# A stack of four graph layers: maps back to node-major on the quarters of the TensorE array, and sums over nodes on four column tiles

## The chip, the cores and the metric

The kernel runs on one core of one Trainium2 chip. The metric is the device time of one execution in microseconds; lower is better. The median of three runs of the kernel before is 1238.32 us (1236.02 to 1239.87). The profile was taken in an execution of 1238.1 us, of which the traced span is 1236.1 us.

## What is computed

The input `x` has 8 batches of 2048 nodes with 64 features in fp32, and `adj` is a 2048x2048 matrix of which each row is divided by its number of entries. Four layers follow each other. Each one takes a layer norm and a ReLU, applies a graph layer, and adds the result to `x`:

```python
h = relu(layernorm(x)); x = x + L0(h, adj)   # Chebyshev convolution: h, adj h, adj adj h with node-wise weights
h = relu(layernorm(x)); x = x + L1(h, adj)   # three steps: v = W2 relu(W1 [v, adj v] + b1) + b2
h = relu(layernorm(x)); x = x + L2(h, adj)   # adj h, scaled per feature, times w_out, plus b_out
h = relu(layernorm(x)); x = x + L3(h, adj)   # attention over adj > 0.5, softmax over nodes, elu
```

Before layer 1 begins, node 0 of `v` is set to a given vector (`L1_gnn_intervention_value`). Where no entry of `adj` is above 0.5, which is the case with these inputs, the attention of layer 3 comes out uniform, and the layer is a mean over all nodes and an elu of it. The kernel's main path is made for that case. A test of that case runs beside the other work; a general path stands behind a flag and isn't entered here.

## The kernel before

Two batches are held side by side, so that one item is a pair of batches: 2 x 64 features fill the 128 partitions or columns of a tile. There are four items (`NP`), and each is cut in four blocks of 512 nodes (`NB`). The pattern of the adjacency lies in SBUF for the whole run as `BT`.

Data has two forms. *Node-major* tiles hold 128 nodes on the partitions, four such groups in a block, and the 128 features of the pair in the columns. *Feature-major* tiles hold the 128 features on the partitions and 512 nodes in the columns. The big product (`product`, L245 to L256) goes from node-major to feature-major: for each of 16 chunks of nodes it multiplies a high and a low half of the data (`halves`, L225) with `BT`, 32 matmuls of 128x512 that all add up in one PSUM bank. The layers run 4 items x 4 blocks of it in several stages. `fill` puts other TensorE work after chosen chunks.

`back_to_nodes` (L661) goes from feature-major to node-major and applies a 64x64 weight matrix to both batches on the way. The weight tile `wmat` is 128x128 with the same 64x64 matrix in two corners on the diagonal and zeros elsewhere. For each of the four groups of 128 nodes the feature-major tile is the stationary operand and `wmat` the moving one. It is called

- in `prepare_next` (L672) for each block of an item that enters layer 1 (16 calls, PSUM tile `bn_u`): a block of `h` is loaded, in block 0 node 0 is overwritten with `ivt` (L681, a copy of one row on ScalarE), the block is transposed, copied to SBUF, mapped back and split into halves;
- in `finish` of `layer1` (L876) for each block of each of the three steps (48 calls, `bn`);
- in `finish2` of `layer2` (L946) for each block (16 calls, `bn`).

Another small map of layer 1, `map_two` (L894, PSUM tile `ph`), stays feature-major. It already addresses the four 64x64 quarters of the array, with one product of 512 columns on each.

`sums` (L957) is the mean of layer 3: for each block it multiplies the four groups of 128 nodes by a 128x128 matrix of ones, 16 products for an item, all adding up in one PSUM tile `pS`. `outputs` (L969) then makes the elu and the final add.

All products of these parts are fp32; each appears in the trace as two matmul records with a weight load each. A scheduling layer orders the instructions of each engine from the program's order, priorities and dependences; `tc.issue_after(x)` makes it put an instruction behind `x` on its engine. [...]The order on ScalarE matters for one point of the change: the copy of `ivt` into the next item's block (L681), the ReLU of a block in layer 1 (L918), the copies of `ph` (L907) and the casts in `halves` (L230) share its queue.

PSUM tiles come from three tags with two buffers each: `big` (two banks), `mm` and `tr` (one bank).

Of the kernel before, what the change touches and what calls it, by code (L numbers as in the profile page):

```python
# [8 lines left out]
F32 = mybir.dt.float32  # L9
# [4 lines left out]
AF = mybir.ActivationFunctionType  # L14
ALU = mybir.AluOpType
# [27 lines left out]
def uniform_path(  # L43
# [30 lines left out]
    nc = tc.nc  # L74
    P = 128
    B, N, C = x.shape
    NP = B // 2
    NCH = N // P
    NB = N // 512
# [6 lines left out]
    psums = [pro.enter_context(tc.tile_pool(name="psump", bufs=1, space=bass.MemoryType.PSUM))]  # L86
# [14 lines left out]
    def bank(tag, name):  # L101
        return psums[-1].tile([P, 512], F32, tag=tag, name=name)
# [11 lines left out]
    ones = consts.tile([P, P], F32, name="ones")  # L114
# [19 lines left out]
    def nodes(acc):  # L134

        return acc.rearrange("p j f -> p (j f)").rearrange("p (e j c) -> p j e c", e=2, c=C)

    def load_x(layer, p, nb, queue=nc.sync):
        acc = block("acc", f"acc_{layer}_{p}_{nb}", 2)
        fill_x(acc, layer, p, nb, queue)  # L140
        return acc
# [6 lines left out]
    def load_h(p, nb, name, pool):  # L148
        t = pool.tile([P, 4, 2 * C], F32, tag="hb", name=f"hb_{name}", bufs=2 if lastp else 3)
        (nc.sync if lastp else nc.scalar).dma_start(t, hs[p][:, part(nb), :])  # L150
        return t
# [9 lines left out]
    def split(t):  # L161
        return t.rearrange("p j (b c) -> p j b c", b=2)
# [8 lines left out]
    squares, lows, stored = [], [], []  # L171
# [50 lines left out]
    copies = []  # L222
    lastp = []

    def halves(src, name, pool=None, later=None):  # L225

        pool, bufs = (work, 6) if pool is None else (pool, 4)
        Hq = pool.tile([P, 4, 2 * C], F32R, tag="H", name=f"H_{name}", bufs=bufs)
        Lq = pool.tile([P, 4, 2 * C], F32R, tag="L", name=f"L_{name}", bufs=bufs)
        copies.append(nc.scalar.copy(Hq, src))  # L230
        def rest():
            lows.append(nc.vector.tensor_tensor(Lq, src, Hq.bitcast(F32), op=ALU.subtract))

        rest() if later is None else later.append(rest)
        return Hq, Lq
# [29 lines left out]
    def to_feat(h, out, name):  # L265
        pt = transposed(lambda t: h[:, t, :], name)
        nc.scalar.copy(out, pt.rearrange("p t n -> p (t n)"))
        return out
# [7 lines left out]
    def term(k, name):  # L276
        pool = l0t if k == 1 else l0f[0]
        return pool.tile([P, 512], F32, tag=f"t{k}", name=name, bufs=(2, 4, 1)[k])
# [286 lines left out]
    nm = "0_1_3a"  # L565
    tx = work.tile([P, 512], F32, tag="z", name=f"t1T_{nm}", bufs=3)
    ps = bank("b1", f"bv_{nm}")
    for m in range(NCH):
        if m in (2, 7, 12):
            go_back(1 + m // 5)  # L570
        for i in range(2):
            nc.tensor.matmul(
                ps, hls[1][m // 4][i][:, m % 4, :], BT[:, m, 3 * 512:],
                start=(m == 0 and i == 0), stop=(m == NCH - 1 and i == 1),
# [32 lines left out]
    b1c = consts.tile([P, 1], F32, name="b1c")  # L607
    b1s = consts.tile([P, 1], F32, name="b1s")
# [43 lines left out]
    w1e = consts.tile([P, P], F32, name="w1e")  # L652
    ivt = consts.tile([1, P], F32, name="ivt")

    def feat(i, name):

        if i == 0:
            return term(1, name)
        return lastp[0].tile([P, 512], F32, tag="fm", name=name, bufs=4)

    def back_to_nodes(fT, wmat, name, tag="big"):  # L661

        ps = psums[-1].tile([P, 4, 2 * C], F32, tag=tag, name=f"bn_{name}")
        for t in range(4):
            nc.tensor.matmul(ps[:, t, :], fT[:, t * P:(t + 1) * P], wmat, start=True, stop=True)  # L665
        return ps


    items = [(1, p) for p in range(NP)] + [(2, p) for p in range(NP)]
    ops = {}  # L670

    def prepare_next(n, q):  # L672
        if n >= len(items):
            return
        layer, p = items[n]
        nm = f"{layer}_{p}_{q}"
        hl, gT = ops.setdefault(n, ([], []))
        h = load_h(p, q, nm, lastp[0] if n else l0q)
        if layer == 1:
            if q == 0:  # L680
                nc.scalar.copy(h[0:1, 0, :], ivt)  # L681
            gT.append(to_feat(h, feat(0, f"gT_{nm}"), nm))
            h = back_to_nodes(gT[q], w1e, f"u_{nm}", "big" if n else "mm")
        hl.append(halves(h, nm))

    def rows4(r):
        return r.rearrange("p (b c) -> p b c", b=2)[:, None].to_broadcast([P, 4, 2, C])
# [47 lines left out]
    for p in range(NP):  # L735
# [47 lines left out]
        for nb in range(NB):  # L783
            nm = f"0_{p}_{nb}b"
# [4 lines left out]
                tag="mm" if p + nb else "b0",  # L789
# [32 lines left out]
    w1vT, w1eT, w2T, wos, w1v2, w1e2, r1e, rbo = (wl[:, i, :] for i in range(8))  # L822
# [46 lines left out]
    def layer1(n, p):  # L869
        hl, gT = ops[n]  # L870
        steps = 3
        for s in range(steps):
            last = s == steps - 1
            g_new, hl_new = [], []

            def finish(nb):  # L876
                nm = f"1_{p}_{s}_{nb}"
                if last:
                    acc = load_x(1, p, nb)
                    pn = back_to_nodes(g_new[nb], w2T, nm)  # L880
                    nc.vector.tensor_tensor(nodes(acc), split(pn), nodes(acc), op=ALU.add)
                    keep(p, nb, acc, f"2_{p}_{nb}", rows4(rbo))
                else:
                    pn = back_to_nodes(g_new[nb], w1e2, nm)
                    nc.vector.tensor_tensor(split(pn), split(pn), rows4(r1e), op=ALU.add)
                    hl_new.append(halves(pn, nm))

            def mid():
                if last:
                    prepare_next(n + 1, 2)  # L890
                else:
                    finish(2)

            def map_two(nb):  # L894

                ph = psums[-1].tile([P, 2, 512], F32, tag="big", name=f"ph_1_{p}_{s}_{nb}")
                w = w1v2 if s else w1vT
                two = (slice(0, C), slice(C, P))
                for i in range(2):
                    for bb in range(2):  # L900
                        nc.tensor.matmul(  # L901
                            ph[two[bb ^ i], bb, :], w[two[bb], two[bb]], gT[nb + i][two[bb], :],
                            start=True, stop=True,
                        )
                for i in range(2):
                    for bb in range(2):
                        nc.scalar.copy(gT[nb + i][two[bb], :], ph[two[bb ^ i], bb, :])  # L907

            for nb in range(NB):
                nm = f"1_{p}_{s}_{nb}"  # L910
                crow = load_crow(nb, nm)
                g = feat((s + 1) % 2, f"g_{nm}")
                fill = {8: mid} if nb == 3 else {}
                if nb % 2 == 0:
                    fill[10] = lambda: map_two(nb)
                product(hl, nb, nm, g, crow, fill=fill)
                gadd = nc.vector.tensor_tensor(g, g, gT[nb], op=ALU.add)
                nc.scalar.activation(g, g, AF.Relu, bias=b1s if s else b1c)  # L918
                g_new.append(g)
                go_on()  # L920
                if nb in (1, 2):
                    finish(nb - 1)
                    if last:
                        prepare_next(n + 1, nb - 1)
                if s < 2:
                    k = 2 * (8 * p + 4 * s + nb)
                    with tc.issue_after(gadd.ins):
                        test(k)
                        test(k + 1)
            if last:  # L930
                finish(2)
                prepare_next(n + 1, 3)
            if last and n == NP - 1:

                put_off.append(lambda: finish(3))
            else:
                finish(3)
            gT, hl = g_new, hl_new
# [4 lines left out]

    accs, es, zs, pS = [], [], {}, {}

    def finish2(g):  # L946
        p, nb = divmod(g, NB)
        nm = f"acc_2_{p}_{nb}"
        acc = term(1, nm) if p % 2 else feat(1, nm)
        acc = acc.rearrange("p (j f) -> p j f", j=4)  # L950
        accs.append(acc)
        fill_x(acc, 2, p, nb)
        pn = back_to_nodes(es[g], wos, f"2_{p}_{nb}")
        nc.vector.tensor_tensor(nodes(acc), split(pn), nodes(acc), op=ALU.add)
        norm_relu(acc, f"3_{p}_{nb}", lambda h: zs.update({g: h}))

    def sums(g):  # L957
        p, nb = divmod(g, NB)
        if nb == 0:
            pS[p] = bank("tr", f"pS_{p}")  # L960
        for t in range(4):
            nc.tensor.matmul(  # L962
                pS[p][:, :2 * C], ones, zs[g][:, t, :],
                start=(nb == 0 and t == 0), stop=(nb == NB - 1 and t == 3),
            )
        if nb == NB - 1:
            outputs(p)

# [648 lines left out]
```

## Time and profile before

| | |
|---|---|
| time, median of 3 | 1238.32 us |
| span of the trace | 1236.1 us |
| TensorE busy | 1197.7 us, 97% |
| VectorE busy | 744.7 us, 60% |
| ScalarE busy | 237.0 us, 19% |
| GpSimd busy | 223.5 us, 18% |
| matmul records | 5798 |
| granted TensorE clock, mean | 0.993 of full |

A page of the profile lists engines with busy time, the span in slices, DMA queues, the chain of work that ended last, and groups of instructions: line, engine, operation, output and inputs, partitions x elements, count, busy time and mean of one, and the idle time of the engine before them with what ended it. Matmuls are pipelined, so the busy time of a group of matmuls is more than what it adds to the queue. What a group adds is read from the starts of the matmuls around it. In the timeline each row has its start, its time, engine, line and operation; equal neighbours are merged.

By time, layer 0 runs until about 630 us (its last products with the node-wise weights), layer 1 until about 1087 us (its last map back), and layer 2 with the sums of layer 3 to the end; each overlaps a little with the next.

### The profile page before, as it was taken

What the parts mean: (1) busy time and instruction counts of PE and PEld (TensorE: products, weight loads), DVE (VectorE), ACT (ScalarE), POOL (GpSimd) and SP (SyncE); (2) the same over time, 40 slices, a digit from 0 to 9 for tenths busy, and PEclk for the clock granted to TensorE, in tenths of its full rate; (3) what the DMA queues carried; (4) which work ended last, traced back from release to release, by engine and by line L of the source; (5) the groups of instructions that cost most, each with busy time, mean ns of one, the idle gap of its engine ahead of it and who ended that gap; (6) DMA issues with size and microseconds to landing.
All of it is one profiled execution on the core that took longest, in us unless ns stands there. A gap on an engine that the chain in (4) does not pass through costs nothing.

```text
span 1236.1 us, 15662 instructions
## 1 busy us (share of the span) xinstructions
PE 1197.7 (97%) x5798; PEld 843.7 (68%) x5798; DVE 744.7 (60%) x1940; ACT 237.0 (19%) x377; POOL 223.5 (18%) x233
## 2 busy tenths in 40 slices
PE   5899999999999999999989999999999999999995
PEld 4675555555675557655557787787877877888884
DVE  5456888777757774477654436444644545566664
ACT  6610001000010000000022233233223223211100
POOL 5410222211131111011110013003101400331211
PEclk9999999999999999999999999999999999999997
DMA  9951334332332233122256526543743563533311
GB/s 355 379 154 47 102 105 115 84 86 77 90 102 73 64 82 85 54 64 64 60 128 126 134 85 156 132 85 123 158 115 92 154 131 92 155 124 112 119 58 40
DMA packets 100985, 140.99 MB, mean 114 GB/s; under 512 B 43772, under 2 KB 58108, under 8 KB 98852
## 3 DMA queue, kind: packets, MB, share of 16 engines
q1 hardware_dynamic: 82820, 80.74, 24.9%
q0 software_dynamic: 11776, 48.15, 12.9%
q10 hardware_dynamic: 6304, 11.01, 2.8%
q8 instruction: 48, 0.79, 0.3%
q14 instruction: 37, 0.30, 0.1%
HBM read 95.03 MB, written 35.66 MB: 106 GB/s over the span
## 4 chain that ended last, share of the span: by engine, by line
PE 92%; DMA 3%; DVE 3%; issue 1%; POOL 1%; ACT 0%; SPq 0%; POOLq 0%; ACTq 0%
PE bv L250 38%; PE y L711 26%; PE bn L665 5%; PE bv_1b L250 2%; PE bv_3b L250 2%; PE bv_2b L250 2%; PE bv_0b L250 2%; PE ph L901 2%; DMA BT<-in_adj_dram 2%; PE bn_u L665 1%; PE bv_0a L250 1%; PE bv_3a L250 1%; PE pt L262 1%; PE bv_2a L250 1%; PE pS L962 1%; PE bv_1a L250 1%
## 5 line engine op out<-in xcount | busy, mean ns | idle before, releaser
L250 PE MATMUL bv<-BT,H 128*128 128x512 f32 x1024 | 409.7, 400 | 0.0
L250 PE MATMUL bv<-BT,L 128*128 128x512 f32 x1024 | 401.3, 392 | 0.0
L250 PEld LDWEIGHTS bv<-BT,H 128*128 128x128 f32 x1024 | 193.0, 188 | 56.6 <-issue 19.5
L250 PEld LDWEIGHTS bv<-BT,L 128*128 128x128 f32 x1024 | 193.0, 188 | 37.0
L720 DVE SCALAR_TENSOR_TENSOR acc<-y,emb,acc 128x128 f32<-128x128 f32 x512 | 176.3, 344 | 65.7 <-PE y L711 65.7
L720 DVE SCALAR_TENSOR_TENSOR odd<-y,emb,odd 128x128 f32<-128x128 f32 x448 | 153.4, 343 | 0.0
L711 PE MATMUL y<-wt,t0T 64*128 64x512 f32 x512 | 143.7, 607 | 2.4 <-DVE odd L720 1.7
L194 POOL TENSOR_TENSOR rstd<-var,mhalf 128x8 f32<-128x8 f32 x64 | 105.7, 1653 | 182.4 <-DVE var L191 181.0
L240 DVE TENSOR_TENSOR g<-bv,crow 128x512 f32<-128x512 f32 x48 | 33.2, 691 | 173.0 <-PE bv L250 173.0
L186 ACT ACTIVATE sq<-z 128x512 f32<-128x512 f32 x64 | 40.4, 631 | 398.0 <-DVE z L181 388.1
L711 PEld LDWEIGHTS y<-wt,t0T 64*128 64x128 f32 x512 | 45.8, 185 | 63.3 <-issue 57.1
L692 POOL TENSOR_TENSOR acc<-acc,b2r 128x512 f32<-128x512 f32 x16 | 22.2, 1389 | 315.7 <-DVE z L181 315.7
L692 POOL TENSOR_TENSOR acc<-acc,wl 128x512 f32<-128x512 f32 x16 | 20.5, 1283 | 295.8 <-DVE z L181 295.8
L711 PE MATMUL y<-wt,t1T 64*128 64x512 f32 x256 | 66.7, 589 | 0.0
L197 DVE SCALAR_TENSOR_TENSOR z<-z,rstd 128x512 f32<-128x512 f32 x64 | 44.7, 703 | 35.2 <-POOL rstd L194 35.2
L665 PEld LDWEIGHTS bn<-wl,g 128*128 128x128 f32 x384 | 49.8, 193 | 7.5 <-issue 3.0
L665 PE MATMUL bn<-wl,g 128*128 128x128 f32 x384 | 51.5, 277 | 2.6 <-issue 2.6
L189 DVE TENSOR_REDUCE var<-sq 128x8 f32<-128x512 f32 x64 | 43.6, 681 | 15.6 <-ACT sq L186 15.6
L846 DVE SCALAR_TENSOR_TENSOR junk<-mt,cols,st 128x512 uint8<-128x512 bf16 x64 | 47.7, 745 | 2.7 <-DMA mt<-MD 2.3
L907 ACT COPY g<-ph 64x512 f32<-64x512 f32 x64 | 37.2, 581 | 49.6 <-PE ph L901 48.8
L711 PEld LDWEIGHTS y<-wt,t1T 64*128 64x128 f32 x256 | 27.1, 187 | 27.8 <-issue 27.8
L181 DVE TENSOR_TENSOR z<-acc,mean 128x512 f32<-128x512 f32 x56 | 38.3, 692 | 6.0 <-DMA hs<-z 4.6
(213 smaller groups left out, 1649.7 us busy)
## 6 DMA issues: line engine op xcount, KB each, us to landing
BT<-in_adj_dram POOLq DMA_DIRECT2D x16, 1024.0 KB, 19.6
crow<-crowD SPq DMA_DIRECT2D x64, 256.0 KB, 3.4
st<-in_adj_dram SPq DMA_DIRECT2D x64, 256.0 KB, 3.5
hs<-z POOLq DMA_DIRECT2D x40, 256.0 KB, 3.1
xs<-acc POOLq DMA_DIRECT2D x32, 256.0 KB, 2.4
MD<-BT POOLq DMA_DIRECT2D x16, 512.0 KB, 5.6
acc<-xs SPq DMA_DIRECT2D x32, 256.0 KB, 3.9
hb<-hs SPq DMA_DIRECT2D x28, 256.0 KB, 3.5
```

What stands on the lines that cost most here:

```text
L181: firsts.append(nc.vector.tensor_tensor(split(z), nodes(xt), each(mean)[:, :, :, None].to_broadcast([P, 4, 2, C]), op=ALU.subtract))
L186: squares.append(nc.scalar.activation(sq, z, AF.Square))
L189: nc.vector.tensor_reduce(var, groups(sq), axis=AX.X, op=ALU.add)
L194: powers.append(nc.gpsimd.tensor_tensor(rstd, var, mhalf, op=ALU.pow))
L197: scales.append(nc.vector.scalar_tensor_tensor(groups(h), g, 0.0, rstd[:, :, None].to_broadcast([P, 8, C]), op0=ALU.max, op1=ALU.mult))
L250: nc.tensor.matmul(ps, hl[m // 4][i][:, m % 4, :], BT[:, m, nb * 512:(nb + 1) * 512], start=(m == 0 and i == 0), stop=(m == NCH - 1 and i ...
L665: nc.tensor.matmul(ps[:, t, :], fT[:, t * P:(t + 1) * P], wmat, start=True, stop=True)
L692: nc.gpsimd.tensor_tensor(nodes(acc), nodes(acc), more, op=ALU.add)
L711: nc.tensor.matmul(y[:, bb, :], terms[k][hs_, ts], wt[hs_, k, dg * 512:(dg + 1) * 512], start=(k == 0), stop=(k == K - 1),)
L720: last = nc.vector.scalar_tensor_tensor(xj, yd, ec, old, op0=ALU.mult, op1=ALU.add)
L846: nc.vector.scalar_tensor_tensor(junk, mt, cols[:, i, :], st, op0=ALU.mult, op1=ALU.not_equal, accum_out=bad[:, i, q:q + 1],)
L907: nc.scalar.copy(gT[nb + i][two[bb], :], ph[two[bb ^ i], bb, :])
```

## The change

It replaces the 128x128 form of the map back. Since the weight matrix is zero outside its two corners, half of each full product multiplies zeros. The new `back_to_nodes` gives each quarter of the array a 64x64x64 product: the row half is the batch, the column half is a half of the 128 nodes. The two batches go to two banks of a `big` tile, and the result is handed out as a view with the batch as its own axis. `halves` and the adds in `finish` and `finish2` take that view. For item 0 the old form stays as `back_whole`, in a tile of the tag `mm`.

The sums over nodes use four column tiles of 32 columns: each of the four groups of 128 nodes is multiplied by 32 columns of ones on its own tile, so each tile keeps its own partial sum on 32 partitions of `pS`. At the end of an item one row of each of the four is added up by a product with `sel`, a matrix that has ones in the rows 0, 32, 64 and 96; a VectorE copy `four` brings `pS` to SBUF for that. For the last item this is done one block early, and the last block is added with the old form.

A third edit concerns order: the copy of `ivt` into the next item's block is put behind the newest ReLU of layer 1 on ScalarE.

```diff
-    def back_to_nodes(fT, wmat, name, tag="big"):
-        ps = psums[-1].tile([P, 4, 2 * C], F32, tag=tag, name=f"bn_{name}")
+    two = (slice(0, C), slice(C, P))
+    def back_to_nodes(fT, wmat, name):
+        ps = psums[-1].tile([P, 2, 512], F32, tag="big", name=f"bn_{name}")
+        for t in range(4):
+            for hf in range(2):
+                for bb in range(2):
+                    at = t * P + hf * C
+                    nc.tensor.matmul(
+                        ps[two[hf], bb, t * C:(t + 1) * C],
+                        fT[two[bb], at:at + C], wmat[two[bb], two[bb]], start=True, stop=True,
+                    )
+        return ps[:, :, :4 * C].rearrange("p b (t c) -> p t b c", c=C)
+    def back_whole(fT, wmat, name):
+        ps = bank("mm", f"bn_{name}").rearrange("p (t f) -> p t f", t=4)
         for t in range(4):
             nc.tensor.matmul(ps[:, t, :], fT[:, t * P:(t + 1) * P], wmat, start=True, stop=True)
         return ps
...
+    relus = []
...
             if q == 0:
-                nc.scalar.copy(h[0:1, 0, :], ivt)
+                with tc.issue_after(relus[-1].ins) if relus else nullcontext():
+                    nc.scalar.copy(h[0:1, 0, :], ivt)
             gT.append(to_feat(h, feat(0, f"gT_{nm}"), nm))
-            h = back_to_nodes(gT[q], w1e, f"u_{nm}", "big" if n else "mm")
+            h = (back_to_nodes if n else back_whole)(gT[q], w1e, f"u_{nm}")
...
-                nc.scalar.activation(g, g, AF.Relu, bias=b1s if s else b1c)
+                relus.append(nc.scalar.activation(g, g, AF.Relu, bias=b1s if s else b1c))
...
+    sel = lastp[0].tile([P, P], F32, name="sel")
+    nc.gpsimd.memset(sel, 0.0)
+    for q in range(0, P, 32):
+        nc.gpsimd.memset(sel[q:q + 1, :], 1.0)
...
+        final = g + 1 == NP * NB
         if nb == 0:
             pS[p] = bank("tr", f"pS_{p}")
-        for t in range(4):
-            nc.tensor.matmul(
-                pS[p][:, :2 * C], ones, zs[g][:, t, :],
-                start=(nb == 0 and t == 0), stop=(nb == NB - 1 and t == 3),
-            )
+        if not final:
+            for t in range(4):
+                nc.tensor.matmul(
+                    pS[p][32 * t:32 * t + 32, :2 * C], ones[:, :32], zs[g][:, t, :],
+                    start=(nb == 0), stop=(nb == NB - 1 or g + 2 == NP * NB),
+                )
+        if nb == NB - 1 or g + 2 == NP * NB:
+            if not final:
+                four = lastp[0].tile([P, 2 * C], F32, name="four")
+                nc.vector.tensor_copy(four, pS[p][:, :2 * C])
+                pS[p] = bank("tr", f"pS4_{p}")
+                nc.tensor.matmul(
+                    pS[p][:, :2 * C], sel, four, start=True, stop=(nb == NB - 1)
+                )
+            else:
+                for t in range(4):
+                    nc.tensor.matmul(
+                        pS[p][:, :2 * C], ones, zs[g][:, t, :], start=False, stop=(t == 3)
+                    )
```

## Prediction

> **What bounds the kernel now.** I read the shares of busy time first, then the chain of work that ended last, to see whether the busiest engine is also the path.
>
> ```profile
> PE 1197.7 (97%) x5798; PEld 843.7 (68%) x5798; DVE 744.7 (60%) x1940; ACT 237.0 (19%) x377; POOL 223.5 (18%) x233
> ...
> PE 92%; DMA 3%; DVE 3%; issue 1%; POOL 1%; ACT 0%; SPq 0%; POOLq 0%; ACTq 0%
> ```
>
> It is: 92% of the chain is TensorE, in program order. A microsecond off TensorE's queue after layer 0 is a microsecond off the time, until something else ends last; VectorE at 60% leaves room. The groups by shape say what the change touches.
>
> ```profile
> L665 PE MATMUL bn<-wl,g 128*128 128x128 f32 x384 | 51.5, 277 | 2.6 <-issue 2.6
> ...
> L665 PE MATMUL bn_u<-w1e,gT 128*128 128x128 f32 x128 | 18.0, 284 | 0.7 <-ACT gT L267 0.7
> L962 PE MATMUL pS<-z,ones 128*128 128x128 f32 x128 | 18.0, 286 | 5.4 <-DVE z L197 5.3
> L901 PE MATMUL ph<-g,wl 64*64 64x512 f32 x128 | 17.4, 614 | 0.0
> L665 PE MATMUL bn<-wl,e 128*128 128x128 f32 x128 | 16.9, 275 | 0.0
> ```
>
> 384+128+128 records are 80 calls of the map back, eight each (an fp32 product leaves two records, its passes). Busy times of pipelined matmuls overlap, so I price a group by what it adds between matmuls of the big product, which step by 0.2285 us (20 take 4.56 or 4.57 us in the chain).
>
> ```profile
> 658.65 0.39 PE L250 MATMUL bv<-BT,L 128*128 128x512 f32 x1
> 658.89 1.05 PE L665 MATMUL bn<-wl,g 128*128 128x128 f32 x8
> 659.69 0.48 PE L250 MATMUL bv<-BT,H 128*128 128x512 f32 x1
> 660.01 0.40 PE L250 MATMUL bv<-BT,L 128*128 128x512 f32 x1
> ```
>
> 660.01 − 658.65 − 2×0.2285 = **0.90 us** for a map back now: eight passes 0.111 us apart, and no switching cost. The nearest row to the new form is the kernel's other map, already on the four 64x64 quarters:
>
> ```profile
> 655.13 0.39 PE L250 MATMUL bv<-BT,L 128*128 128x512 f32 x1
> 655.45 1.09 PE L901 MATMUL ph<-gT,wl 64*64 64x512 f32 x8
> 656.47 0.50 PE L250 MATMUL bv<-BT,H 128*128 128x512 f32 x1
> 656.80 0.39 PE L250 MATMUL bv<-BT,L 128*128 128x512 f32 x1
> ```
>
> 656.80 − 655.13 − 0.457 = **1.21 us**, and all 24 of these groups read 1.215. Each quarter streams two passes of 512 columns; such a pass is 0.427 us (the row-tiled products of L711 step by 0.429). So 0.854 us is streaming and **0.36 us** is entering and leaving the quarters: in the trace the first weight load starts 0.09 us after the last full-array stream is over instead of ahead of it, and the next full-array load starts only after the last quarter has drained.
>
> Do four quarters really run at once?
>
> ```profile
> 655.45 0.21 PEld L901 LDWEIGHTS ph<-gT,wl 64*64 64x64 f32 x8 [0.35 <-issue]
> ```
>
> Eight weight loads of 0.13 us end within 0.21 us. In the trace neighbouring quarters start 7 ns apart and a quarter's second load 55 ns after its first, so yes.
>
> The last view is the one long stall in this part of the span, on ScalarE and then TensorE:
>
> ```profile
> 635.55 2.37 ACT L907 COPY gT<-ph 64x512 f32<-64x512 f32 x4 [1.85 <-PE ph L901]
> 646.75 0.30 ACT L681 COPY hb<-ivt 1x128 f32<-1x128 f32 x1 [8.83 <-DMA acc<-xs]
> 646.96 1.33 ACT L918 ACTIVATE g<-g,b1c 128x512 f32<-128x512 f32 x2
> ```
>
> ```profile
> 644.80 0.39 PE L250 MATMUL bv<-BT,L 128*128 128x512 f32 x1
> 647.77 0.46 PE L665 MATMUL bn<-wl,g 128*128 128x128 f32 x2 [2.59 <-issue]
> ```
>
> ScalarE stands 8.8 us at L681, a one-row copy for the next item that waits for loads. Behind it is a ReLU (L918) whose input was ready from 639.85 on (the end of L917); the map back waits for that ReLU.
>
> [...]after the stall TensorE runs at 0.57 in 648 to 652.
>
> **The change, part by part.**
>
> *Maps back.* Sixteen 64x64 products instead of four 128x128. Four calls keep the old form (item 0), 76 change. Each quarter gets four products, eight passes of 64 columns. Bounds for a pass: 53 ns (half of 107, the streaming part of today's 111), if quarters never disturb each other; 111 ns, if two quarters take turns. I take 57 ns: half of 111 plus the few ns that every step shows beyond its stream. A group is then 0.36 + 8×0.057 = **0.82 us**. By the changed kernel's order of instructions:
> - 60 stand between big products (6 of them ahead of transposes): 60×(0.897−0.82) = 4.6.
> - 9 follow a transpose and cost 0.968 today, 0.075 of it waiting for ScalarE's copy; the drain now covers that wait: 9×0.148 = 1.3.
> - 3 pairs (layer 1's `bn_u` directly ahead of `bn`) share one visit: 1.857 − (0.36 + 16×0.057) = 0.58 each, 1.7.
> - The last lies in the tail, where VectorE's chain of layer norms sets the pace: 0.
>
> Sum **−7.6 us**. Their readers (L885, L881, L954, the copy L230) take the same 512 elements a partition from two banks; nothing for it, VectorE and ScalarE are off the path.
>
> *Sums over nodes.* Four column tiles of 128x32, each one product of 128 columns in two passes: 0.36 + 2×0.107 = 0.58 instead of 0.90. 13 such groups lie between big products: 13×0.32 = −4.2. Each item then needs a copy (`four`) and a product with `sel`. In the order of instructions three of them stand four big matmuls after the sums: 3×0.23 of streaming. VectorE has the scaling (L240, 0.69) and the copy (0.28, as L973) to finish in those 0.9 us; with the drain that is 0.2 late each: 3×0.2. Sum −4.2 + 1.3 = **−2.9 us**. In the tail the copy for the last item stands on VectorE between L954 and the mean, on the path: **+0.3**; its product with `sel` runs while TensorE is idle anyway.
>
> *The one-row copy.* It now waits for the newest ReLU, so in item 0's first step nothing blocks L918. From 644.80 to the first undisturbed matmul at 651.73 are 6.93 us; seven steps and a map would be 7×0.2285 + 0.90 = 2.50. That is **−4.4 us**, half clock included. The price: the copy, the transposes and `bn_u` of the three later items now stand behind the ReLU of block 1 in step 2. Before, at 719.68 (the last matmul ahead of L665), that ReLU ended 3.0 us later (721.98 + 0.72) and the copy adds 0.3; TensorE arrives at the transposes after 0.23 + 0.82 + 7×0.2285 = 2.65 us. So 0.6 of waiting, three times: **+1.9 us**. Queued behind the transposes is the big product; nobody else waits.
>
> Sum: −7.6 −2.9 +0.3 −4.4 +1.9 = −12.7, from 1238.3 to **1225.6 us**.
>
> **Rivals.**
> 1. *The switch eats the tiling.* A pass of 67 ns would make a map as dear as today (0.36 + 8×0.067 = 0.90). For it: 64 instructions a map where no train of them exists yet; against: the 7 ns starts. Left are half the pairs and waits (−1.9), the sums, the stall: −1.9 −2.9 +0.3 −4.4 +1.9 = −7.0, **1231**.
> 2. *Quarters that share rows take turns* once passes are as short as loads. A map is 0.36 + 16×0.057 = 1.27: 60×0.37 + 9×0.30 + 3×0.33 = +26; column tiles likewise, 13×(0.36 + 8×0.107 − 0.90) + 1.3 = +5.5; less 4.4, plus 2.2: **1268**, slower. [...]Against: in `ph` four loads overlapped fully.
> 3. *No new waits*: VectorE in time for `sel`, the ReLU early enough: 2.5 better, **1223**.
>
> **Chances.** Forecast 0.60, rival 3 0.14, rival 1 0.14, rival 2 0.12. The range reaches from 1219 (rival 3 with a pass of 53 ns, 60×8×0.004 = 1.9, and a cheaper visit) to 1236 (rival 1 with sums no cheaper than today); rival 2 and slivers are outside. Faster: forecast, rival 3 and most of rival 1, 0.82; same 0.06; slower 0.12.
>
> **What would show it.** `bn` as 32 records a map on 64*64, a group adding 0.82 us; `pS` groups adding 0.58; no idle near 645 and no slow slice there; ScalarE's L681 copies after L918 and a wait of the transposes for them; `sel` products waiting briefly for `four`. The prediction is wrong if a map adds over 0.9 us, or if the stall near 645 only changes its owner, such as a load that the first map itself needs.

## Result and the profile after

The changed kernel takes **1225.16 us** (median of 4 runs, 1223.90 to 1226.44) where the kernel before takes 1238.53: a ratio of 0.9894, 95% interval 0.9874 to 0.9915. A second series gave 0.9905 (0.9890 to 0.9920). The forecast was 1225.6. The profiled span went from 1236.1 to 1224.5 us.

The shares of busy time and the chain of the page after, the same lines that opened the prediction:

```profile
PE 1186.0 (97%) x7630; PEld 801.6 (65%) x7630; DVE 744.6 (61%) x1944; ACT 237.6 (19%) x377; POOL 224.6 (18%) x238
...
PE 90%; DVE 4%; DMA 3%; issue 1%; ACT 1%; POOL 1%; SPq 0%; POOLq 0%; DVEq 0%; ACTq 0%
```

TensorE still sets the end. It has 1832 more matmul records and is busy 11.7 us less. The groups by shape for the lines that changed:

```profile
L674 PE MATMUL bn<-wl,g 64*64 64x64 f32 x1536 | 33.2, 224 | 0.0
L674 PE MATMUL bn<-wl,e 64*64 64x64 f32 x512 | 11.1, 224 | 0.4 <-DVE e L241 0.4
L674 PE MATMUL bn_u<-w1e,gT 64*64 64x64 f32 x384 | 8.3, 224 | 0.5 <-ACT gT L268 0.5
```

1536 + 512 + 384 records are 76 maps of 32. The mean of one record, 224 ns, says little, since they overlap; what a map costs is again in the starts around it. The timeline of TensorE after, one map:

```profile
647.15 0.39 PE L251 MATMUL bv<-BT,L 128*128 128x512 f32 x1
647.47 0.69 PE L674 MATMUL bn<-wl,g 64*64 64x64 f32 x32
...
648.43 0.39 PE L251 MATMUL bv<-BT,L 128*128 128x512 f32 x1
```

648.43 − 647.15 − 2×0.2285 = **0.82 us**, against 0.90 before. All 53 maps that stand alone between big products read 0.824 to 0.833. Now a sum over nodes:

```profile
1134.13 0.39 PE L251 MATMUL bv<-BT,L 128*128 128x512 f32 x1
1134.45 0.43 PE L993 MATMUL pS<-z,ones 128*32 128x128 f32 x8
...
1135.14 0.39 PE L251 MATMUL bv<-BT,L 128*128 128x512 f32 x1
```

1135.14 − 1134.13 − 0.457 = **0.55 us**. Before, a sum over nodes added 1144.10 − 1142.74 − 0.457 = **0.90 us**:

```profile
1142.74 0.40 PE L250 MATMUL bv<-BT,L 128*128 128x512 f32 x1
1142.98 1.05 PE L962 MATMUL pS<-z,ones 128*128 128x128 f32 x8
1143.79 0.48 PE L250 MATMUL bv<-BT,H 128*128 128x512 f32 x1
1144.10 0.40 PE L250 MATMUL bv<-BT,L 128*128 128x512 f32 x1
```

Last, ScalarE at the place of the long stall (the copies of `ph`, then the ReLU that L681 had held up by 8.8 us):

```profile
637.90 2.38 ACT L927 COPY gT<-ph 64x512 f32<-64x512 f32 x4 [1.86 <-PE ph L921]
642.29 0.72 ACT L938 ACTIVATE g<-g,b1c 128x512 f32<-128x512 f32 x1 [2.01 <-issue]
```

The one-row copy is no longer between them, and TensorE runs on undisturbed (busy throughout 640 to 660, granted clock 1.00). The price appears where the copy now stands, in the transposes of the next item:

```profile
719.48 0.39 PE L251 MATMUL bv<-BT,H 128*128 128x512 f32 x1
720.31 0.66 PE L263 MATMUL pt<-ident,hb 128*128 128x128 f32 x4 [0.44 <-ACT hb L702]
```

One thing blurs whole spans. In these two traces layer 1 begins 2.35 us later after than before (first L186 at 635.41 against 633.06), and this moves from run to run, in layer 0, which the change doesn't touch: a second trace of the changed kernel has a span of 1221.9. So I also give three stretches read from TensorE's records: layer 1 (first `ph` to the product `pf`), layer 2 (from there to the last big product), and the rest up to TensorE's last matmul. They repeat: that second trace (e11 below) gives the same to 0.01 us.

| kernel | time, us | ratio to before (95%) | layer 1 | layer 2 | rest |
|---|---|---|---|---|---|
| before | 1238.5 | | 438.53 | 142.46 | 11.01 |
| changed | 1225.2 | 0.9894 (0.9874–0.9915) | 429.40 | 138.04 | 10.84 |
| e1 no order edit | 1228.6 | 0.9918 (0.9904–0.9932) | 434.90 | 138.04 | 10.84 |
| e2 maps only | 1232.7 | 0.9950 (0.9938–0.9962) | 433.64 | 141.61 | 10.74 |
| e3 order only | 1235.7 | 0.9973 (0.9967–0.9980) | 435.12 | 142.46 | 11.00 |
| e4 sums only | 1234.2 | 0.9965 (0.9953–0.9977) | 438.62 | 138.90 | 11.07 |
| e5 quarter by quarter | 1288.2 | 1.0415 (1.0390–1.0439) | 477.66 | 152.09 | 11.44 |
| e6 older ReLU | 1224.6 | 0.9897 (0.9880–0.9914) | 429.09 | 138.04 | 10.85 |
| e7 one visit | 1219.6 | 0.9870 (0.9848–0.9891) | 424.83 | 138.04 | 10.85 |
| e8 sums behind map | 1226.1 | 0.9910 (0.9893–0.9926) | 429.40 | 140.06 | 10.63 |
| e9 together | 1219.8 | 0.9858 (0.9838–0.9877) | 424.81 | 136.70 | 10.63 |
| e10 two per quarter | 1230.8 | 0.9948 (0.9929–0.9966) | 433.11 | 139.19 | 10.83 |
| e11 changed again | 1226.0 | 0.9905 (0.9890–0.9920) | 429.41 | 138.04 | 10.84 |
| e12 three apart | 1216.9 | 0.9827 (0.9812–0.9841) | 422.52 | 136.70 | 10.63 |

From before to changed the three stretches sum to 9.13 + 4.42 + 0.17 = 13.7 us.

### The profile page after: what moved, and what is told of

The parts are those of the page before. It is cut to its first block, busy times and chain, and to the rows that moved or that the text cites. A ratio compares the mean times of both kernels' runs of the same rounds, so it can differ in the third digit from the quotient of the medians.

```text
span 1224.5 us, 19343 instructions
## 1 busy us (share of the span) xinstructions
PE 1186.0 (97%) x7630; PEld 801.6 (65%) x7630; DVE 744.6 (61%) x1944; ACT 237.6 (19%) x377; POOL 224.6 (18%) x238
## 3 DMA queue, kind: packets, MB, share of 16 engines
q10 hardware_dynamic: 6304, 11.01, 2.8%
## 4 chain that ended last, share of the span: by engine, by line
PE 90%; DVE 4%; DMA 3%; issue 1%; ACT 1%; POOL 1%; SPq 0%; POOLq 0%; DVEq 0%; ACTq 0%
PE bv L251 39%; PE y L732 26%; PE bn L674 3%; PE bv_1b L251 2%; PE bv_3b L251 2%; PE bv_2b L251 2%; PE bv_0b L251 2%; DMA BT<-in_adj_dram 2%; PE ph L921 2%; PE bv_0a L251 1%; PE bv_3a L251 1%; PE bv_2a L251 1%; PE bv_1a L251 1%; PE pt L263 1%; DMA x<-in_x_dram 1%
## 5 line engine op out<-in xcount | busy, mean ns | idle before, releaser
L186 ACT ACTIVATE sq<-z 128x512 f32<-128x512 f32 x64 | 40.4, 631 | 396.6 <-DVE z L181 386.6
L938 ACT ACTIVATE g<-g,b1s 128x512 f32<-128x512 f32 x32 | 23.2, 724 | 99.1 <-DVE g L937 98.9
L712 POOL DMA_DIRECT2D hs<-z x32 | 18.6, 582 | 126.8 <-DVE z L197 90.2
```

The source lines that it names most:

```text
L186: squares.append(nc.scalar.activation(sq, z, AF.Square))
```

## Experiments

### The three edits one by one

My theory was the prediction's: maps, sums and the order edit each bring their own share, and the shares add up. The main rival: one of them does the work and the others only move waits.

**Without the order edit (e1).**

```diff
-                with tc.issue_after(relus[-1].ins) if relus else nullcontext():
-                    nc.scalar.copy(h[0:1, 0, :], ivt)
+                nc.scalar.copy(h[0:1, 0, :], ivt)
```

> The changed kernel (1225.2 us) without its third edit: the one-row copy of ivt stands again where the planner puts it. Theory A (the edit takes away a stall of 4.4 us near 645 us and charges about 1.2 us of waiting transposes): 3.2 us longer than the changed kernel, about 1228.4, with an idle TensorE near 645 us, a one-row copy of some 8 us of waiting ahead of the ReLU, and no wait of pt for the copy. Theory B (the stall belonged to loads that the maps or the sums moved as well): same time as the changed kernel, 1225.2, no stall.

Measured: 1228.6. The stall is back, as ScalarE's timeline of e1 shows:

```profile
648.96 0.30 ACT L701 COPY hb<-ivt 1x128 f32<-1x128 f32 x1 [9.11 <-DMA acc<-xs]
649.16 1.33 ACT L937 ACTIVATE g<-g,b1c 128x512 f32<-128x512 f32 x2
```

So the stall belongs to the place of that copy, not to the maps. By medians e1 is 3.5 us longer than the changed kernel, near the 3.2 expected. The profiled execution was the longest of the six, 1231.3 us; in it layer 1 is 5.5 us longer, and the windows of e1 show most of why (columns: the window, its length, then PE, PEld, DVE, ACT and POOL busy with their instructions, then the granted clock, DMA share and GB/s):

```profile
650.00:654.00 4.00, 4.00 (x39) 3.30 (x40) 2.71 (x6) 1.08 (x2) 0.00 (x0) 0.50 1.23 265
654.00:658.00 4.00, 4.00 (x14) 3.13 (x14) 0.00 (x0) 0.00 (x0) 0.00 (x0) 0.71 0.88 259
```

From the last big product ahead of the stall to the first one after it are 4.32 us, in the trace of before 4.36, but in e1 12 steps of the big product then run at half clock, against 5 before, 4 in e2 and 2 in e4. Counted in each trace like the prediction's 4.4, the stall with what follows costs 4.4 (before), 4.6 (e2 and e4) and 5.8 us (e1). Another 1.2 us lies in waits of `bn_u`, which come up again below.

Half clock lasts 3.41 us in the traces of before (from 648.13 on), e2 and e4, and 6.83 us in e1 (from 649.50 on). The idle stretch ahead of it was 2.6 to 3.2 us in these four traces. A map back takes up a part of the half clock, too: in e4 1.7 us of it pass from the start of the map to the next big product, and only 2 steps are left. Why half clock lasted longer in e1 was not shown.

**Maps only (e2), order only (e3), sums only (e4)**: each is the kernel before with the lines of one edit of the diff.

> The kernel before with the quarter maps alone: old sums, old place of the one-row copy. Theory A (maps: 60 groups 0.072 us cheaper each, nine bn_u 0.138, three pairs 0.35): -4.3 -1.2 -1.0 = -6.5, about 1232. Theory B (the maps gave nothing or lost, and the sums or the order edit carry the gain): 1237 to 1240.

> The kernel before with only the one-row copy put behind the newest ReLU. Theory A: -4.4 (stall and slow clock gone) + 1.2 (transposes wait for the copy) = -3.2, about 1235.3. Theory B (with the old maps the first map back waits for something else near 645 us, such as the ReLU's own inputs): 0 to -1, about 1238.

> The kernel before with only the sums over nodes on four column tiles. Theory A: 13 groups 0.345 us cheaper = -4.5, three products with sel +0.7, the copy in the tail +0.15: -3.65, about 1234.9. Theory B (column tiles keep VectorE's z for longer or sel waits): -1 to -2, about 1237.

Measured: −6.2, −3.3 and −4.7 us by medians against 1238.9 in the same series; −6.0, −3.4 and −3.4 by the stretches. Each is what its theory A gave, within the interval; the rivals that put the gain in one edit fall. Layer 2 is additive to the hundredth: −0.85 (e2) and −3.57 (e4) make −4.42, and the changed kernel has −4.42. In layer 1 −4.89 (e2) and −3.41 (e3) make −8.30 of −9.13. The 0.8 left over is mainly an overlap of two waits: in e2, as in e1, the nine `bn_u` add 8.6 us, among them 1.2 of waiting for ScalarE's copy `gT`; in the changed kernel, where the transposes ahead of them wait already, they add 7.5.

### Why the maps gain so little: the price of a visit

By the prediction, which read it from the groups of `ph` in the trace of before, 0.36 of a map's 0.82 us is entering and leaving the quarters. If that is paid per visit, two groups of the same mode next to each other pay it once.

**One visit for two maps (e7).** In 20 of its 24 places `map_two` is put directly behind a map back:

```diff
-                if nb % 2 == 0:
+                if nb == 0 and s == 0:
                     fill[10] = lambda: map_two(nb)
...
                     finish(nb - 1)
+                    if nb == 1:
+                        with tc.issue_after(mapped[-1].ins):
+                            map_two(2)
...
             gT, hl = g_new, hl_new
+            if not last:
+                with tc.issue_after(mapped[-1].ins):
+                    map_two(0, s + 1, gT)
```

> The changed kernel with the other map on quarters, ph, put directly behind a map back bn in 20 of its 24 places, so that both share one visit to the 64x64 mode. Theory A (0.36 us is the price of entering and leaving the mode, paid once per visit): 20 x 0.36 = 7.2 shorter, about 1218, less what ScalarE's copies of ph (2.4 us) hold up. Theory B (the price is paid per group, at each start of a new accumulation or bank, whatever stands next to it): 0, 1225.

The timeline of TensorE in e7:

```profile
644.06 0.39 PE L251 MATMUL bv<-BT,L 128*128 128x512 f32 x1
644.38 0.69 PE L675 MATMUL bn<-wl,g 64*64 64x64 f32 x32
644.89 1.04 PE L922 MATMUL ph<-gT,wl 64*64 64x512 f32 x8
...
646.20 0.39 PE L251 MATMUL bv<-BT,L 128*128 128x512 f32 x1
```

646.20 − 644.06 − 0.457 = 1.68 us for both, in all 17 places where the pair stands alone, against 0.825 + 1.215 = 2.04 apart: 0.358 saved, so the price is per visit, and theory B falls. Layer 1 is 4.6 us shorter, not 7.2: in the other three places the next item's transposes stand directly behind the pair, without big products between, and TensorE reaches them before the newest ReLU and the one-row copy behind it are done:

```profile
PE pt L263 <- ACT hb L703: 3.5, 3, 1.4
```

(The waits of e7: total us, times, longest.)

**From one tiled mode into another (e8).** The sums, 128x32 tiles, directly behind a map on 64x64 tiles:

```diff
                 finish2(g - 1)
+            if g > 1:
+                with tc.issue_after(mapped[-1].ins):
+                    sums(g - 2)
...
-            if g > 1:
-                fill[15] = lambda: sums(g - 2)
```

> The changed kernel with the sums over nodes (128x32 column tiles) put directly behind a map back (64x64 quarters) instead of ten chunks later. Theory A (going from one tiled mode to the other costs no more than one drain): one of two exits and entries is saved, 13 x 0.15 to 0.36 = 2 to 4.7 shorter, 1220.5 to 1223. Theory B (a change between two tiled modes costs as much as leaving for the full array and coming back): 0, 1225.

```profile
1082.94 0.39 PE L251 MATMUL bv<-BT,L 128*128 128x512 f32 x1
1083.26 0.69 PE L675 MATMUL bn<-wl,e 64*64 64x64 f32 x32
1083.88 0.43 PE L994 MATMUL pS<-z,ones 128*32 128x128 f32 x8
...
1084.58 0.40 PE L251 MATMUL bv<-BT,L 128*128 128x512 f32 x1
```

1084.58 − 1082.94 − 0.457 = 1.18, against 0.825 + 0.554 = 1.38 apart. So a change between two shapes of tile costs about 0.16 of the 0.36, and 0.196 is saved in each of the ten places without a wait, within what theory A gave. The kernel still is no faster than the changed one, because the sums now come too early in four places. The waits of e8:

```profile
PE pS L994 <- DVE z L197: 3.9, 4, 1.0
```

By the starts these four groups are 4.2 us longer than the others, 14 × 0.196 = 2.7 is saved, and one more sum than in the changed kernel lies ahead of the last big product (0.55): layer 2 is 2.0 longer, the rest 0.2 shorter.

### Do the quarters really overlap?

**Quarter by quarter (e5).** The same sixteen products of a map, in another order:

```diff
-        for t in range(4):
-            for hf in range(2):
-                for bb in range(2):
+        for hf in range(2):
+            for bb in range(2):
+                for t in range(4):
```

> The changed kernel with the sixteen products of a map in another order: all four of one quarter behind each other, then the next quarter. Same products, same results. Theory A (products are started in the order of the queue, so only neighbours in the queue overlap): a map adds 0.36 + 32 x 0.058 = 2.2 us instead of 0.825, 76 maps, about +105 us, 1330. Theory B (products of another quarter are taken ahead from the queue[...], so two quarters overlap): a map adds about 1.3, +36, 1261. Theory C (order within a map does not matter): 0, 1225.

```profile
644.16 0.39 PE L251 MATMUL bv<-BT,L 128*128 128x512 f32 x1
644.48 1.54 PE L674 MATMUL bn<-wl,g 64*64 64x64 f32 x32
...
646.29 0.40 PE L251 MATMUL bv<-BT,L 128*128 128x512 f32 x1
```

A map adds 646.29 − 644.16 − 0.457 = 1.67 us: twice the changed kernel's, and between theories A (2.2) and B (1.3); C falls. It is a loss of the kind that rival 2 of the prediction stood for, brought about by the order alone. The starts of single records show where it arises. Counted from the last big product ahead of the map, the eight records of the first quarter start at 318, 425, 483, 542, 600, 658, 717 and 775 ns, and the second quarter starts at 606, 6 ns behind the first one's fifth record (the first of its third product) and ahead of its fourth product (717), which stands earlier in the program. So the second quarter starts 288 ns behind the first, where in the changed kernel neighbouring quarters start 6.6 to 7 ns apart. A map takes 0.845 us more than in the changed kernel. What holds the second quarter back for that time was not shown.

**Two per quarter (e10).**

```diff
-        for t in range(4):
-            for hf in range(2):
-                for bb in range(2):
+        for tt in range(0, 4, 2):
+            for hf in range(2):
+                for bb, t in ((0, tt), (0, tt + 1), (1, tt), (1, tt + 1)):
```

> The changed kernel with two products (four matmul records) of one quarter behind each other before the next quarter, twice round. Theory A ([...]as the quarter-by-quarter run suggested: the next quarter began right after the fifth of eight records): four in a row never hold up the queue for long, a map adds 0.04 us more, 0.865, and the time is 3 us longer, 1228. Theory B[...]: 0.33 us more a map, 25 us longer, 1250. Theory C (the trouble is any two products of one quarter in a row): in proportion to the run with four in a row, about half of its 64 us, 1257.

Measured: a map adds 0.882 where the changed kernel's adds 0.825, and the three stretches are 4.9 us longer. So theories B and C fall. Of the 0.057 us, theory A expected 0.04. In the starts each of the other three quarters has a step of 99 ns instead of 58 in its second round, ending at 713, 726 and 739: the second quarter's third product starts at 614 ns, 14 behind the first quarter's third at 600, and its second record 99 ns later. What lengthens that step was not shown.

### The waits for ScalarE

**An older ReLU (e6).**

```diff
-                with tc.issue_after(relus[-1].ins) if relus else nullcontext():
+                with tc.issue_after(relus[-2].ins) if relus else nullcontext():
```

> The changed kernel with the one-row copy behind the last but one ReLU instead of the newest. Theory A (the stall near 645 us stays away, and the transposes no longer wait for the copy): -1.2, about 1224.0, no wait of pt for hb. Theory B (the copy then waits for its loads again and blocks the newest ReLU in item 0): stall back, +3, 1228.

The stall stays away and the transposes no longer wait, yet layer 1 is only 0.3 us shorter. The wait has moved one instruction on. The waits of e6:

```profile
PE bn_u L674 <- ACT gT L268: 1.4, 6, 0.6
```

In the changed kernel this line reads 0.5, in three waits. The transposes come earlier (716.85 in the trace of e6, where those of the changed kernel start at 720.31), but ScalarE's copy `gT` behind them comes only after the ReLU: the ReLU starts at 718.20, `gT` at 718.83, and `bn_u` at 719.45.

**All three moves together (e9)**: e6 and e7, and e8 in the places without a wait.

> The changed kernel with three moves together: ph directly behind a map back in 20 places, the one-row copy behind the last but one ReLU, and the sums over nodes directly behind a map back in the 9 places where the run with sums_behind_map showed no wait for z. Theory A (a visit to a tiled mode is paid once, with 0.358 us saved where both share the 64x64 mode and 0.196 where the shape of the tile changes; the transposes behind ph no longer wait 1.4 us for the copy): 20 x 0.358 + 9 x 0.196 = 8.9 shorter than the changed kernel, plus 0.6 for a wait of bn_u: about 8.3, 1217. Theory B (what ScalarE cannot finish in time for the merged groups comes out as another wait of the same size): no faster than ph behind a map alone, about 1220.5.

Measured: 6.1 us shorter than the changed kernel by the stretches, not 8.3. The groups and `pt` are as expected (1.682, 1.183, no wait of `pt`), and once more the wait has moved. Layer 1 is as long as in e7 (424.81 against 424.83), so there theory B held: what the older ReLU took from `pt` came back at `bn_u`. The gain over e7 is that of the sums. ScalarE, then TensorE, in e9:

```profile
719.52 1.15 ACT L928 COPY g<-ph 64x512 f32<-64x512 f32 x2
720.70 0.59 ACT L268 COPY gT<-pt 128x512 f32<-128x512 f32 x1
```

```profile
721.33 0.69 PE L675 MATMUL bn_u<-w1e,gT 64*64 64x64 f32 x32 [1.68 <-ACT gT L268]
```

**Three maps left apart (e12)**: as e9, but in the three places ahead of transposes `map_two` stays where it was. The edit is shown against e9.

```diff
-                if nb == 0 and s == 0:
+                apart = last and p < NP - 1
+                if (nb == 0 and s == 0) or (nb == 2 and apart):
                     fill[10] = lambda: map_two(nb)
...
-                    if nb == 1:
+                    if nb == 1 and not apart:
```

> The run with the three moves together, but with the three ph that stood ahead of the next item's transposes left in their own place as in the changed kernel, so that ScalarE's 2.4 us of copies from ph no longer lie between those transposes and bn_u. Theory A (the 4.5 us of extra cost of the three bn_u came from those copies): 4.5 - 0.6 (the wait of bn_u seen with the older ReLU) - 3 x 0.358 = 2.8 shorter than together, some 9 shorter than the changed kernel, about 1217. Theory B (bn_u waits for something else, such as the one-row copy's own loads): the same time as together, 1219.8.

Measured: 1216.9, ratio 0.9827, and 2.3 us less in layer 1 than e9. The nine `bn_u` fall from 12.0 to 8.6 us and three merges of 0.358 are given up: −3.4 + 1.1 = −2.3. So the copies of `ph` were the cause. This version beats both kernels: 8.4 us below the changed one by the stretches.

**The changed kernel again (e11)** served as the reference for e9 and e10.

> The changed kernel itself, for comparison on the same chip: 0.9894 of the kernel before, 1225.

Measured: 0.9905, 1226.0.

## Why the prediction was right

The total was right, −13.4 measured by medians (−13.7 by the stretches) against −12.7, with the mechanism it named. By its steps:

- **A map at 0.82.** Right: 0.825. The chosen 57 ns a pass is 58.3 in the trace, steady over four quarters, and 0.36 for a visit is confirmed by e7's 0.358. The prediction's 0.427 us for a pass of 512 columns and 107 ns for 128 were estimates; in the trace of before such passes step by 0.429 us (L711) and by 108 to 112 ns (L665, L262), and behind `ph` the first full-array weight load starts at 656.47, 0.52 us after the last quarter's second record. Rivals 1 (67 ns) and 2 (quarters in turn) fall with it. For the groups between big products 4.6 was forecast; read from the starts it is 3.74 (50 maps, 0.075 each in the mean) + 1.04 (9 maps that share their group with transposes, 0.115 each) + 0.27 (the one ahead of `pf`) = 5.05. Part of it was not in the forecast: eight of the 50 cost 0.938 before, since their first load waited for the ReLU, and cost 0.825 now.
- **Nine `bn_u`.** 0.830 instead of 0.82: −1.2 for −1.3. That nothing is left of the wait for `gT` (0.075 us each before) holds only because the first transposes already wait for the one-row copy; in e2, without that wait, `bn_u` waits 1.2 us and this gain is nearly gone.
- **Three pairs.** Mis-sized: 1.51 measured, 1.27 forecast, so −1.0 for −1.7. The shared visit is there, but TensorE now reaches `bn_u` 0.2 us ahead of the copy `gT`: the 0.5 us in three waits behind `bn_u` among the groups above.
- **Sums.** 0.554 for 0.58: −4.5 for −4.2. The products with `sel` cost the 0.23 of their streaming; the 0.2 of waiting put on each didn't occur, VectorE had `four` ready. Together −3.8 for −2.9.
- **`four` in the tail.** 0.1 for 0.3: the mean (L179) starts at 1207.08, 0.16 us after the add ahead of the copy ended, where it starts 0.03 after at the other blocks. The copy starts 0.05 us ahead of the end of that add, and the mean 0.08 ahead of the end of the copy. The last map, which the forecast put at 0, makes the rest 0.27 us shorter in e2. So the rest as a whole is 0.17 shorter, where +0.3 was forecast.
- **The stall.** −4.4 as forecast, shown by e1 and e3. As a size it is the least certain, since the half clock behind it lasted 3.4 us in three traces and 6.8 in a fourth.
- **The price of the order edit.** +1.9 forecast, three times 0.6. Measured: the waiting transposes add 1.25 us in total, 0.65 ahead of the first of these items and 0.30 ahead of each of the other two. The forecast read the distance to the ReLU ahead of the first and took it three times. With the old maps, in e3, the waits are 0.60, 0.25 and 0.25: the reading fits the first and not the others. Another 0.15 was not foreseen: in these places the transposes no longer share a group with a map. Rival 3 (no new waits) was right for `sel` and wrong here.

So the forecast was too favourable in the pairs (0.7) and `bn_u` (0.1), and too unfavourable in the maps (0.4), the sums (0.9), the price of the order edit (0.5) and the tail (0.5). One thing it didn't have at all: the steps of the big product between the groups add up to 0.6 us more than before, half clock set aside; why was not tested. Together that is 0.9 of the 1.0 us between −12.7 and −13.7, and that the errors had both signs helped.

## What to carry to other kernels

In this kernel a small product on the quarters of the array paid 0.358 us for the visit, so shortening its passes from 111 to 58 ns brought little (0.90 to 0.82), and putting two tiled groups beside each other brought more at each place (0.358) than the tiling did (0.075). In another kernel measure the price of a visit first. Order the products so that neighbours in the queue are on different tiles: here two in a row on one tile cost 0.057 us a map, four in a row 0.845. After every such move look at who waits for the evacuation: three times here a wait that was taken from one instruction came back on the next one behind the same ScalarE queue.

## What the runs showed that was not expected

- A visit to 64x64 tiles costs 0.358 us, and two groups that stand next to each other pay it once (e7); going on to 128x32 tiles within it costs about 0.16 (e8).
- With four products in a row on one quarter the second quarter starts at 606 ns, behind the first one's fifth record (600), and a map adds 1.67 us instead of 0.825 (e5). With two in a row it adds 0.882 (e10).
- Trains of 64-column products on four quarters keep 58.3 ns a record in each quarter, with quarters 6.6 to 7 ns apart, so the four together start a record every 15 ns (the changed kernel).
- After an idle stretch of 2.6 to 3.2 us the granted clock was half for 3.41 us in three traces (before, e2, e4) and for 6.83 in a fourth (e1): 5, 4, 2 and 12 steps of the big product were slow behind the same copy.
